# Four graph layers on one core: the small steps of the norms on GpSimd, a two-pass exponential unit, and new ranks

## The chip, the core and the metric

The kernel runs on one core of a Trainium2 chip. The core has a TensorE for matrix products (PE in the profile, with its weight loads shown apart as PEld), a VectorE (DVE), a ScalarE (ACT), a GpSimd (POOL) and a SyncE (SP). The engines run side by side; each works through its own queue of instructions in order, and they wait for each other by semaphores. The metric is the device time of one execution in microseconds (us), as the median of several runs. The profile is of one execution.

## The reference

The input is 16 graphs of 1024 nodes with 128 features each, and a 1024x1024 matrix of edges per graph. Four attention layers follow each other. After each one comes a residual sum and a layer norm:

```python
def _layernorm(x, axis=-1, eps=1e-5):
    m = jnp.mean(x, axis=axis, keepdims=True)
    v = jnp.var(x, axis=axis, keepdims=True)
    return (x - m) / jnp.sqrt(v + eps)
...
x = _layernorm(x + _L0_gnn_ref(x, adj, ...), axis=-1)
x = _layernorm(x + _L1_gnn_ref(x, adj, L1_gnn_W, L1_gnn_a), axis=-1)
x = _layernorm(x + _L2_gnn_ref(x, adj, ...), axis=-1)
x = _layernorm(x + _L3_gnn_ref(x, adj, L3_gnn_W, L3_gnn_a), axis=-1)
```

The third of them holds two attention steps, each behind a graph norm, and each ends in an exponential linear unit (elu); the first of the two has eight heads:

```python
def graph_norm(x, alpha, scale, shift, num_features):
    ...
    var = mean_x2 - mean * mean
    xn = (xr - alpha[None, :, None] * mean) / jnp.sqrt(var + EPS)
    xn = scale[None, :, None] * xn + shift[None, :, None]
...
h = graph_norm(x, gn1_alpha, gn1_scale, gn1_shift, nfeat)
h = gat_layer(h, adj, W1, a1, nheads, n_hidden1, concat=True)
h = graph_norm(h, gn2_alpha, gn2_scale, gn2_shift, nhid)
out = gat_layer(h, adj, W2, a2, 1, nhid, concat=False)
```

So each graph passes six norms: four layer norms and two graph norms. Each of them needs one over the root of a variance.

## The kernel before

A graph's 1024 nodes lie on 128 partitions in 8 groups, so that a tile of a whole graph is 128 x 1024 values. The sixteen graphs are sixteen passes through the function `graph(b)`, but nothing runs in the order in which it is written. A recorder (`Recorder`) takes down each operation with its engine, its operands and what it depends on. `Recorder.run` then works through a plan: every operation has a rank, every engine a time at which it is free, and at each step the operation that can start first is taken, with the lowest rank where two can. Operations of up to four graphs (`AHEAD = 3`) may be mixed. For operations made with `either`, such as copies from PSUM, the scaling by a row's factor (`scaled_rows`) or the affine pass of a norm (`affine`), the plan also chooses between ScalarE and VectorE. `Recorder.issue` then writes the instructions down in the planned order, so each engine's queue is fixed before the kernel starts. All these instructions carry line 430 in the profile; they are told apart by the names of their tiles.

The ranks are an operation's place in its graph, plus the graph's number times `STEP`, plus corrections from tables: `SHIFT` (by place in the graph), `OWN` (by graph and place), `ENDS` (by graph), `LATER` and `LAST` (a handicap on choosing one engine over the other). The plan uses an estimate of each operation's cost (`cost_of`); an arithmetic step on GpSimd of n elements per partition stands there with 200 + 2n ns in which the engine is held.

The places that the change touches:

- `rstd_of` computes one over a root for n variances per partition: ScalarE's Ln and Exp give a first value in `rs_r` (or in `last`, for the last norm of a graph), and three VectorE steps on `rs_q` refine it. It serves all six norms.
- `layernorm` (tiles `ln_m`, `ln_d`, `ln_v`, `shift`) stands behind the first and the third layer. From the statistics of each row in `mv`, which VectorE's bn_stats writes for the two halves of a row, it makes mean and variance in five VectorE steps, calls `rstd_of`, makes `shift` and hands over to eight affine passes.
- `layernorm_centred`, behind the second and the fourth layer, takes sums of squares `ss` from ScalarE, calls `rstd_of` and scales. In the last graph the fourth layer's is split into three pieces.
- The first graph norm (tiles `mvg`, `ga`, `gb`, 128x1) has four VectorE steps after `rstd_of`; the second (tiles `mom`, `var`, `ga8`, `gb8`, 128x8, which appear as `ga` and `gb` in the profile) has two ahead of it and four after it.
- The exponential unit of the eight heads works on `h2`, one 128 x 1024 tile per graph.

Between the norms lie the wide operations of VectorE, 128 x 1024 or 128 x 512 each: the products of weights and mask (`weights_of`: `row<-row,ratio,maskT`), the comparisons of the eight heads (`row<-row,ns`, which either engine can do), their masking (`row<-row,maskT`) and the sums over PSUM (`x<-bank`).

GpSimd has next to no arithmetic in this kernel. Its queue carries 36 DMA issues: eight that load the first two graphs' edges, and for each of the other fourteen graphs one that brings the edges over as bf16 (`adj<-in_adj_dram`) and one that loads the turned mask into its place (`maskT<-up`). The queue of SyncE carries the other transfers.

Of the kernel before, what the change touches and what calls it, by code (L numbers as in the profile page):

```python
# [21 lines left out]
P = 128  # L22
# [419 lines left out]
def gnn_stack_kernel(ctx: ExitStack, tc: tile.TileContext, w: dict, out: bass.AP):  # L442
# [11 lines left out]
    def fast_path(stack):  # L454
# [70 lines left out]
        for count in (1, D):  # L525
            eps[count] = const([P, 1], f"eps{count}")
            nc.vector.memset(eps[count], count * EPS)
# [81 lines left out]
        def rstd_of(var, n, r=None, count=1):  # L609

            if r is None:
                r = small("rs_r", P, n)
            q = small("rs_q", P, n)
            rc.scalar.activation(r, var, AF.Ln, bias=eps[count])
            rc.scalar.activation(r, r, AF.Exp, scale=-0.5)
            rc.vector.scalar_tensor_tensor(q, var, count * EPS, r, ALU.add, ALU.mult)
            rc.vector.scalar_tensor_tensor(q, q, -0.5 * count**0.5, r, ALU.mult, ALU.mult)
            rc.vector.scalar_tensor_tensor(r, q, 1.5 * count**0.5, r, ALU.add, ALU.mult)
            return r
# [4 lines left out]
        def layernorm(y, bs, r=None):  # L624
            twice, apart, var = (small(k, P, G) for k in ("ln_m", "ln_d", "ln_v"))
            rc.vector.tensor_tensor(twice, bs[:, :, 1], bs[:, :, 4], ALU.add)
            rc.vector.tensor_tensor(apart, bs[:, :, 1], bs[:, :, 4], ALU.subtract)
            rc.vector.scalar_tensor_tensor(apart, apart, D / 4.0, apart, ALU.mult, ALU.mult)
            rc.vector.tensor_tensor(var, bs[:, :, 2], bs[:, :, 5], ALU.add)
            rc.vector.tensor_tensor(var, var, apart, ALU.add)  # L630
            r = rstd_of(var, G, r, count=D)
            shift = small("shift", P, G)
            rc.vector.scalar_tensor_tensor(shift, twice, -0.5, r, ALU.mult, ALU.mult)
            for g in range(G):
                affine(y[:, g, 0:D], y[:, g, 0:D], r[:, g : g + 1], shift[:, g : g + 1])
# [206 lines left out]
        def graph(b):  # L842
# [147 lines left out]
            rc.vector.tensor_mul(ga, r, gn1[1])  # L990
            rc.vector.tensor_mul(gb, mv[:, 0:1], gn1[0])
            rc.vector.tensor_mul(gb, gb, ga)
            rc.vector.tensor_sub(gb, gn1[2], gb)
# [133 lines left out]
            rc.scalar.activation(e, h2, AF.Exp)  # L1127
            rc.vector.tensor_scalar(e, e, 1.0, -1.0, ALU.min, ALU.add)
            rc.vector.tensor_tensor(h2, h2, e, ALU.max)
# [12 lines left out]
            rc.vector.tensor_mul(var, mom[:, 0, :], mom[:, 0, :])  # L1142
            rc.vector.tensor_sub(var, mom[:, 1, :], var)
# [3 lines left out]
            rc.vector.tensor_mul(ga, r, gn2[:, 1, :])  # L1147
            rc.vector.tensor_mul(gb, mom[:, 0, :], gn2[:, 0, :])
            rc.vector.tensor_mul(gb, gb, ga)
            rc.vector.tensor_sub(gb, gn2[:, 2, :], gb)  # L1150
# [59 lines left out]
        for b in range(B):  # L1210
# [6 lines left out]
        LATER = {"vector": (122, -69, 156), "scalar": (66, -208, -6827)}  # L1217
        SHIFT = (
            3, 0, 12, -14, -124, -168, -37, -11, 130, -700, -702, -314, 104, 102, -282, -141, -150, -37, -23, -27,
            21, 27, 12, -23, 6, 47, 87, 193, 224, -183, -20, -6, 390, -479, -81, -387, 48, 56, 154, -4330,  # L1220
        )
        OWN = (
            (-1898, -1727, -871, -373, -2236, -1762, -2185, -2227, -1860, 872, -624, -909, 177, 153, -623, -117, 558, 649, -286, -733, -82, -35, 163, 158, 6, 62, -280, -413, -74, 85, -88, 244, -310, -830, -1150, -1555, -1749, -1397, -1363, -2273),
            (-740, -395, -86, 141, -113, -170, -67, -413, -471, -2323, -3056, -3903, -754, -1217, -892, -93, 644, 659, 392, 154, 484, -304, 291, 73, 14, -23, -183, -471, 139, 45, -54, -100, -299, -549, -786, -333, -137, -562, -375, 540),
            (-244, -188, -35, 102, -5, 18, -46, 79, 113, 337, -1213, -146, -286, 163, -81, 192, 583, 988, 78, -104, 5, 106, 140, 49, 23, 257, 76, 143, 1205, -237, 59, 45, 47, -186, -27, -215, -204, 136, 24, 664),
            (-1, 0, 16, 11, -24, -24, -28, -260, -232, -433, -306, -220, -204, -180, -167, -111, -193, -183, 37, 50, 2, 27, 26, 23, 13, 43, 45, 30, -25, 96, -7, -103, 608, 23, 263, 106, -52, 23, 61, 272),
            (8, 8, -6, -6, -13, 32, -7, 30, 30, -51, -38, -600, 5, 4, -23, -3, 15, 4, -15, 14, -5, -7, 12, 34, 131, 69, 68, 180, 31, 35, 101, 76, 9, -284, -291, -342, -367, -67, 11, -60),
            (21, 21, 23, 24, 23, 59, 63, 75, -39, -85, 89, -1235, -1221, -1138, 145, -90, -209, -109, 29, -250, -140, -115, 102, 306, 66, 20, -5, 1, -10, -175, 24, 17, -47, 29, 46, -1093, -356, -62, 11, 1),
            (-4, 5, 0, 0, 0, -97, 0, 68, 80, 30, 86, 56, 111, -25, 293, 134, 135, 49, 110, 128, -398, -290, 32, 33, 120, 13, -7, 18, 24, -21, -168, -163, -3, -87, -45, -77, -3, -9, -39, 16),
            (1, -3, -3, -13, -1, 24, -16, -17, -158, -54, -144, -22, 9, -1, -1, -8, -8, -1, 0, 18, -141, 14, 16, 53, 37, -57, -14, -26, -19, -23, -30, -38, -65, -369, -133, 0, -45, -30, -39, 854),  # L1230
            (0, 0, 0, 9, 1, -16, -53, -52, 298, -27, -45, -240, -93, -304, -296, -272, -246, -194, -192, -109, 9, -42, -47, -27, -29, -63, -11, 2, -1, -11, -58, -39, -20, -21, -223, -231, -324, -376, -417, -116),
            (1, -2, -970, 0, 0, -26, -44, -43, 25, -1104, -1179, -19, -451, -637, -839, -694, -19, 68, 30, 32, -8, -11, -55, 337, 351, -2, 17, 8, 4, -8, 38, 38, -2, -10, -95, -866, -839, -1062, -615, -790),
            (-6, -6, -29, -43, -47, -157, -1, -16, 91, 32, 20, -27, -17, -215, -35, -165, -226, -234, -232, -3, -3, -32, -54, 8, -38, -116, -46, 1, 6, 178, 198, 224, 153, 203, -15, -245, -146, -1139, -1245, -2114),
            (-43, -43, -51, -51, -33, -38, 28, 61, -49, -827, -930, -2108, 334, -4, 75, -41, -23, 21, -37, -63, 52, 49, 53, 9, 50, -80, 28, 41, -57, 66, 57, 20, -141, 112, 31, -668, -705, 338, 347, 421),
            (-20, 20, 6, 1, -12, -7, 78, 11, -39, -704, 10, 55, -41, -269, -66, -188, 41, 54, 19, 14, 67, 141, 47, 28, 12, 7, 11, 25, 35, 51, -7, -38, 7, -5, 256, -18, -189, -885, 89, -471),
            (-318, -303, -137, -102, -154, -319, -2367, -2650, -2247, -1733, -7880, -8504, -1388, -1036, 708, 568, -120, 613, 434, 1065, 5085, 2400, -4970, -3152, 885, 1161, 239, 406, 331, 1441, 4292, 3547, -1664, 709, 4888, 6934, 5929, 5348, 10822, 10232),
# [658 lines left out]
```

## Time and profile before

| what | value |
|---|---|
| median of 3 runs | 2430.28 us (2427.98 to 2431.34) |
| the profiled execution | 2428.53 us, of which the span of the trace is 2426.4 us |
| granted TensorE clock | 0.990 |
| VectorE, three-input products `row<-row,ratio,maskT` 128x1024 | 384 instructions, 469.0 us, 1274 ns each |
| VectorE, masking `row<-row,maskT` 128x2048 uint16 | 256 instructions, 309.1 us, 1213 ns each |
| VectorE, comparisons `row<-row,ns` 128x1024 | 308 instructions, 221.4 us, 741 ns each |
| ScalarE, the same comparisons `row<-row,bs2h` 128x1024 | 716 instructions, 767.5 us, 1142 ns each |
| VectorE, a step of `rstd_of` on 128x8 | 64 instructions, 10.1 us, 158 ns each |
| VectorE, `ln_d<-mv` 128x8 | 32 instructions, 5.3 us, 165 ns each |
| GpSimd, 128x1 copy | 2 instructions, 184 ns each |

A page of the profile gives for each engine its busy time, the share of the span and the number of instructions, then the span in 40 slices with the busy share in tenths. Three slices' lines of that page:

```profile
PE   8999999999999999999999999999999999999987
ACT  5597876949679596877859689596876959768864
POOL 1000000000000000000000000000000000000000
```

Every slice is about 61 us long. PE shows 9 nearly everywhere, that is 90% or more; ScalarE swings between 5 and 9; GpSimd is busy only in the first slice. A busy PE need not run at its peak, since the ends of matmuls are modelled.

### The profile page before, as it was taken

The numbers are of one execution on the slowest core, as the hardware profiler recorded it, in microseconds if no ns is written. First come the engines' busy times: TensorE is split into PE (matmuls) and PEld (weight loads), VectorE is DVE, ScalarE is ACT, GpSimd is POOL, SyncE is SP. The second block draws the span as 40 slices with busy tenths as digits, with TensorE's granted clock in tenths as the row PEclk, the third lists the DMA queues.
The fourth block names the chain that finished last, engine by engine and source line by source line (L and its number), as shares of the span: only waits on it lengthen the run. The fifth ranks groups of instructions, "written<-read, shape, count | busy, mean of one in ns | idle before, by whom it ended". The sixth has DMA issues, their size and how long they took to land.

```text
span 2426.4 us, 56241 instructions
## 1 busy us (share of the span) xinstructions
PE 2338.0 (96%) x23100; PEld 1995.4 (82%) x23100; DVE 2258.5 (93%) x4858; ACT 1832.5 (76%) x3451; POOL 28.7 (1%) x47
## 2 busy tenths in 40 slices
PE   8999999999999999999999999999999999999987
PEld 5786887969978797887879878798788978879887
DVE  5799998989999999999999999999999999999997
ACT  5597876949679596877859689596876959768864
POOL 1000000000000000000000000000000000000000
PEclk9999999999999999999999999999999999999999
DMA  9560235062072432607135080442605224020200
GB/s 202 115 171 10 80 90 147 10 148 80 19 191 46 120 100 72 165 19 176 50 81 149 29 207 20 111 108 67 170 19 142 77 80 108 17 79 2 71 2 28
DMA packets 215544, 217.20 MB, mean 90 GB/s; under 512 B 126264, under 2 KB 162288, under 8 KB 213488
## 3 DMA queue, kind: packets, MB, share of 16 engines
q1 hardware_dynamic: 197552, 165.30, 23.7%
q0 software_dynamic: 17728, 48.24, 10.5%
q8 instruction: 183, 3.00, 0.5%
q14 instruction: 81, 0.66, 0.1%
HBM read 193.94 MB, written 67.79 MB: 108 GB/s over the span
## 4 chain that ended last, share of the span: by engine, by line
PE 52%; DVE 40%; ACT 4%; issue 3%; DMA 1%; POOL 0%; ACTq 0%; DVEq 0%
PE bank L430 52%; DVE row L430 27%; DVE x L430 6%; ACT row L430 4%; DVE mv L430 1%; DVE m L430 1%; DVE mf L430 1%; DVE bank L430 1%; DMA row<-in_adj_dram 1%; DVE top_all L430 0%; DVE rdens L430 0%; DVE sums L430 0%; DVE rs_q L430 0%; DVE top L430 0%; DVE ln_v L430 0%
## 5 line engine op out<-in xcount | busy, mean ns | idle before, releaser
L430 PE MATMUL bank<-row,row 128*128 128x129 f32 (+1 forms) x9220 | 1421.4, 313 | 19.8 <-DVE row L430 14.0
L430 PEld LDWEIGHTS bank<-row,row 128*128 128x128 f32 x9220 | 1116.5, 192 | 210.2 <-issue 137.9
L430 ACT ACTIVATE row<-row,bs2h 128x1024 fp8e4<-128x1024 f32 x716 | 767.5, 1142 | 0.0
L430 DVE SCALAR_TENSOR_TENSOR row<-row,ratio,maskT 128x1024 f32<-128x1024 f32 x384 | 469.0, 1274 | 2.6 <-PE bank L430 2.4
L430 PEld LDWEIGHTS <-row 128*128 128x128 fp8e4 (+1 forms) x8320 | 413.2, 98 | 53.4 <-issue 24.2
L430 PE MATMUL bank<-m,row 128*128 128x102 bf16 x8192 | 427.6, 208 | 14.0 <-DVE row L430 12.6
L430 DVE TENSOR_TENSOR row<-row,maskT 128x2048 uint16<-128x2048 uint16 x256 | 309.1, 1213 | 1.7 <-ACT row L430 1.6
L430 ACT ACTIVATE row<-bank 128x512 f32<-128x512 f32 x256 | 150.8, 593 | 169.8 <-DVE bank L430 155.7
L430 DVE TENSOR_SCALAR row<-row,ns 128x1024 fp8e4<-128x1024 f32 x308 | 221.4, 741 | 0.0
L430 PE MATMUL bank<-m,maskT 128*128 128x136 bf16 x3072 | 209.5, 225 | 2.4 <-DVE m L430 2.3
L430 PEld LDWEIGHTS <-maskT 128*128 128x128 fp8e4 x3072 | 200.3, 97 | 4.6 <-issue 4.1
L430 DVE COPY_PREDICATED bank<-maskT,bank 128x512 f32<-128x512 uint8 x256 | 175.7, 689 | 29.5 <-PE bank L430 28.4
L430 DVE CUSTOM_DVE_ANT_0 row<-bank,row 128x512 f32<-128x512 f32 x256 | 173.6, 683 | 9.9 <-ACT row L430 8.6
L430 DVE TENSOR_REDUCE x<-bank 128x136 f32<-128x408 f32 x256 | 144.5, 571 | 12.3 <-PE bank L430 11.7
L430 ACT ACTIVATE row<-bank,rdens 128x128 f32<-128x128 f32 x206 | 60.5, 364 | 113.6 <-DVE rdens L430 113.1
L430 ACT ACTIVATE row<-row,top_all 128x1024 f32<-128x1024 f32 x128 | 139.4, 1144 | 4.7 <-DVE top_all L430 4.6
L430 ACT ACTIVATE half<-maskT,minus_half 128x2048 fp8e4<-128x2048 fp8e4 x64 | 127.5, 1996 | 0.2
L430 PE MATMUL bank<-ident,row 128*128 128x128 f32 x643 | 103.2, 285 | 20.6 <-ACT row L430 11.1
L430 PEld LDWEIGHTS bank<-ident,row 128*128 128x128 f32 x643 | 75.5, 143 | 52.3 <-ACT row L430 21.4
L430 ACT ACTIVATE sq<-row 128x128 f32<-128x128 f32 x256 | 76.4, 302 | 45.7 <-DVE row L430 43.2
L430 ACT COPY row<-bank 128x512 f32<-128x512 f32 x125 | 69.2, 580 | 21.4 <-PE bank L430 20.9
L430 DVE TENSOR_TENSOR row<-row,row 128x384 f32<-128x384 f32 (+3 forms) x120 | 69.8, 587 | 5.4 <-ACT row L430 4.6
(200 smaller groups left out, 2195.7 us busy)
## 6 DMA issues: line engine op xcount, KB each, us to landing
row<-s1d SPq DMA_DIRECT2D x128, 512.0 KB
adj<-in_adj_dram POOLq DMA_DIRECT2D x14, 2048.0 KB, 27.7
up<-half SPq DMA_DIRECT2D x112, 256.0 KB
row<-a_d SPq DMA_DIRECT2D x39, 512.0 KB
maskT<-up POOLq DMA_DIRECT2D x14, 1024.0 KB, 10.5
row<-in_x_dram SPq DMA_DIRECT2D x16, 512.0 KB
out_dram<-row SPq DMA_DIRECT2D x15, 512.0 KB
row<-in_adj_dram POOLq DMA_DIRECT2D x8, 512.0 KB, 16.1
```

What stands on the lines that cost most here:

```text
L430: done = getattr(getattr(self.nc, engine), name)(*[real(a) for a in args], **{k: real(a) for k, a in kw.items()})
```

## The change

It has three parts.

1. The small steps of the norms move from VectorE to GpSimd. VectorE's fused steps (`scalar_tensor_tensor`: a scalar operation and then one with a second tensor) become plain products and sums, so there are more of them: `rstd_of` has five in place of three, with a new tile `rs_v`; `layernorm` has seven ahead of `rstd_of` in place of five. For this the variance is now scaled so that `rstd_of` runs with `count=4` in place of `count=D`, with a constant of its own in `eps`. Ln and Exp stay on ScalarE.
2. The exponential unit of the eight heads was Exp on ScalarE and two passes on VectorE (a minimum and a sum, then a maximum). It becomes Relu of the negated value and Exp of the negated result on ScalarE, and one pass on VectorE.
3. All rank tables have new values, with the sizes as before.

```diff
-        for count in (1, D):
+        for count in (1, 4, D):
...
+            held = small("rs_v", P, n)
             q = small("rs_q", P, n)
+            rc.gpsimd.tensor_scalar(held, var, count * EPS, None, ALU.add)
             rc.scalar.activation(r, var, AF.Ln, bias=eps[count])
             rc.scalar.activation(r, r, AF.Exp, scale=-0.5)
-            rc.vector.scalar_tensor_tensor(q, var, count * EPS, r, ALU.add, ALU.mult)
-            rc.vector.scalar_tensor_tensor(q, q, -0.5 * count**0.5, r, ALU.mult, ALU.mult)
-            rc.vector.scalar_tensor_tensor(r, q, 1.5 * count**0.5, r, ALU.add, ALU.mult)
+            rc.gpsimd.tensor_tensor(q, held, r, ALU.mult)
+            rc.gpsimd.tensor_tensor(q, q, r, ALU.mult)
+            rc.gpsimd.tensor_scalar(q, q, -0.5 * count**0.5, 1.5 * count**0.5, ALU.mult, ALU.add)
+            rc.gpsimd.tensor_tensor(r, q, r, ALU.mult)
...
-            rc.vector.tensor_tensor(twice, bs[:, :, 1], bs[:, :, 4], ALU.add)
-            rc.vector.tensor_tensor(apart, bs[:, :, 1], bs[:, :, 4], ALU.subtract)
-            rc.vector.scalar_tensor_tensor(apart, apart, D / 4.0, apart, ALU.mult, ALU.mult)
-            rc.vector.tensor_tensor(var, bs[:, :, 2], bs[:, :, 5], ALU.add)
-            rc.vector.tensor_tensor(var, var, apart, ALU.add)
-            r = rstd_of(var, G, r, count=D)
+            rc.gpsimd.tensor_tensor(apart, bs[:, :, 1], bs[:, :, 4], ALU.subtract)
+            rc.gpsimd.tensor_tensor(var, bs[:, :, 2], bs[:, :, 5], ALU.add)
+            rc.gpsimd.tensor_tensor(apart, apart, apart, ALU.mult)
+            rc.gpsimd.tensor_scalar(var, var, 4.0 / D, None, ALU.mult)
+            rc.gpsimd.tensor_tensor(var, var, apart, ALU.add)
+            rc.gpsimd.tensor_tensor(twice, bs[:, :, 1], bs[:, :, 4], ALU.add)
+            rc.gpsimd.tensor_scalar(twice, twice, -0.5, None, ALU.mult)
+            r = rstd_of(var, G, r, count=4)
             shift = small("shift", P, G)
-            rc.vector.scalar_tensor_tensor(shift, twice, -0.5, r, ALU.mult, ALU.mult)
+            rc.gpsimd.tensor_tensor(shift, twice, r, ALU.mult)
...
-            rc.vector.tensor_mul(ga, r, gn1[1])
-            rc.vector.tensor_mul(gb, mv[:, 0:1], gn1[0])
-            rc.vector.tensor_mul(gb, gb, ga)
-            rc.vector.tensor_sub(gb, gn1[2], gb)
+            rc.gpsimd.tensor_mul(ga, r, gn1[1])
+            rc.gpsimd.tensor_mul(gb, mv[:, 0:1], gn1[0])
+            rc.gpsimd.tensor_mul(gb, gb, ga)
+            rc.gpsimd.tensor_sub(gb, gn1[2], gb)
...
-            rc.scalar.activation(e, h2, AF.Exp)
-            rc.vector.tensor_scalar(e, e, 1.0, -1.0, ALU.min, ALU.add)
-            rc.vector.tensor_tensor(h2, h2, e, ALU.max)
+            rc.scalar.activation(e, h2, AF.Relu, scale=-1.0)
+            rc.scalar.activation(e, e, AF.Exp, scale=-1.0)
+            rc.vector.scalar_tensor_tensor(h2, e, -1.0, h2, ALU.add, ALU.max)
...
-            rc.vector.tensor_mul(var, mom[:, 0, :], mom[:, 0, :])
-            rc.vector.tensor_sub(var, mom[:, 1, :], var)
+            rc.gpsimd.tensor_mul(var, mom[:, 0, :], mom[:, 0, :])
+            rc.gpsimd.tensor_sub(var, mom[:, 1, :], var)
...
-        LATER = {"vector": (122, -69, 156), "scalar": (66, -208, -6827)}
+        LATER = {"vector": (127, -141, 77), "scalar": (76, -220, -8863)}
         SHIFT = (
...
```

The four steps after `rstd_of` in the second graph norm (`ga8`, `gb8`) change in the same way as those of the first. `AHEAD` and `STEP` keep their values.

## The prediction

> **What bounds the kernel now.** I read the page's totals and slices first, then the middle of the span as one stretch, the chain of waits, the groups by shape, and last the timelines of VectorE and GpSimd at two norms and at GpSimd's DMA issues.
>
> ```profile
> PE 2338.0 (96%) x23100; PEld 1995.4 (82%) x23100; DVE 2258.5 (93%) x4858; ACT 1832.5 (76%) x3451; POOL 28.7 (1%) x47
> PE 52%; DVE 40%; ACT 4%; issue 3%; DMA 1%; POOL 0%; ACTq 0%; DVEq 0%
> 180.00:2160.00 1980.00, 1933.22 (x19093) 1640.81 (x19090) 1884.79 (x4031) 1514.81 (x2860) 18.97 (x23) 1.00 0.35 92
> ```
>
> The third line is a stretch's length, then busy PE, PEld, DVE, ACT and POOL. Between 180 and 2160 us PE idles 1980 - 1933 = 47 us and DVE 95 us: two full engines, with ACT a quarter free and POOL empty. The chain that ended last alternates: 52% on PE, 40% on DVE. So DVE time is worth something, but only where DVE heads the chain; I price it at 0.40 and keep 1.0 as the upper end. PE's idle 47 us is about what a better order alone could win there.
>
> **1. What leaves VectorE.** The instruction lists of the two built programs give the counts: DVE 5848 to 5210, POOL 80 to 985, ACT 3536 to 3503, PE and SP unchanged. Removed from DVE are 40 small steps per graph: 9 in each of two layernorms, 3 in each of four further rstd, 4 and 6 in the two graph norms. 16 x 40, and 6 for the last graph's two extra pieces, make 646. Their price is not the mean of some 157 ns:
>
> ```profile
> 1487.29 0.16 DVE L430 TENSOR_TENSOR ln_m<-mv 128x8 f32<-128x8 f32 x1
> 1487.37 0.17 DVE L430 TENSOR_TENSOR ln_d<-mv 128x8 f32<-128x8 f32 x1
> 1487.45 0.25 DVE L430 TENSOR_TENSOR ln_v<-mv 128x8 f32<-128x8 f32 x2
> 1487.62 0.16 DVE L430 SCALAR_TENSOR_TENSOR ln_d<-ln_d 128x8 f32<-128x8 f32 x1
> ```
>
> Columns are start, duration, engine and operation. Starts are 0.08 us apart: each instruction overlaps the next by 0.08. So 646 x 0.08 = 52 us leave DVE, not 101. The exponential unit drops one 128x1024 TENSOR_SCALAR per graph (689 ns by its row, 0.61 net of overlap): 16 x 0.61 = 10 us. Where two engines can do a step, the new ranks choose anew: DVE takes 22 more 128x1024 comparisons (0.66 net each, 15 us), 21 more 128x384 products (0.47, 10 us) and 10 more 128x512 biases (6 us), and gives up 17 casts (11 us) and some copies; together about +19. DVE ends 52 + 10 - 19 = 43 us lighter; on the path 0.40 x 43 = **-17 us** (ends: 0 and -43).
>
> **2. What ScalarE gets.** One more 128x1024 pass per graph (Relu, 1055 ns by the row of the same shape, 16 us in all); against it 22 comparisons and 65 products leave, and casts come: about zero in sum on an engine with a quarter free. As a dependence, Relu and Exp and one DVE pass replace Exp and two DVE passes: 1.06 - 0.69 = +0.37 us per graph, 6 us in all, 0.40 of it **+2 us**.
>
> **3. What GpSimd gets.** The count per graph is 13 steps in each of two layernorms, 5 in each of four rstd, 4 and 6: 56, and 10 for the last graph, so 906 in all. No such step is in this trace. The nearest rows are a 128x1 COPY on POOL, 184 ns, and the same step on DVE, 157 ns; in the empty tail three dependent DVE steps start 0.19 and 0.20 us apart. Alone, a step on POOL should take 0.2 to 0.25 us, and a layernorm that waited 5 us behind wide DVE work (1486.8 to 1491.9) would be done in 3 to 4: POOL's queue is otherwise empty. That is the case for the change. Against it stand these rows:
>
> ```profile
> 1427.68 0.54 POOL L430 DMA_DIRECT2D maskT<-up  x1 [127.89 <-DVE x L430]
> 1428.21 1.27 POOL L430 DMA_DIRECT2D adj<-in_adj_dram  x1
> ...
> 1428.31 0.72 DVE L430 CAST m<-x 128x1088 bf16<-128x1088 f32 x1
> ...
> 1297.87 1.04 POOL L430 DMA_DIRECT2D maskT<-up  x1 [162.09 <-ACT row L430]
> ...
> 1297.38 1.40 DVE L430 TENSOR_SCALAR row<-row,ns 128x1024 fp8e4<-128x1024 f32 x2
> ...
> 1719.90 1.47 POOL L430 DMA_DIRECT2D adj<-in_adj_dram  x1 [0.62 <-issue]
> ...
> 1720.23 1.04 DVE L430 CAST m<-x 128x1088 bf16<-128x1088 f32 x1
> ```
>
> GpSimd's issue of maskT takes 0.54 us where nothing is in the way and that of adj 0.89. The long ones lie on a DVE CAST or TENSOR_SCALAR, and end 0.1 to 0.5 us after it; in the last pair the CAST too is long, 1.04 against a usual 0.72. So the two engines already hold each other up, in both directions.
>
> How often would it strike? CAST and TENSOR_SCALAR of this kind are busy 246 us, 10% of the span. DVE operations that read two SBUF tiles (469.0, 309.1, 41.1, 41.0, 39.9, 39.0 and 35.2 us in their groups) are 974 us, 40%. Whether these collide with a POOL step no row shows, since a DMA issue is not an arithmetic step that reads tiles. I count them in, as the nearer case for a reading step: 50%.
>
> (a) Hold of DVE: half of the steps meet such an operation, and I let each hold the next one for half a COPY: 906 x 0.5 x 0.092 = 42 us, on the path 0.40 x 42 = **+17 us**. Ends: nothing, and every step a whole COPY, 906 x 0.184 = 167 us, at 0.40 67 us.
>
> (b) Lateness of POOL: the 1220 us in question are some 1200 instructions, 1.0 us each; a step that meets one waits half of it: 906 x 0.5 x 0.5 = 227 us, 2.4 us for each of 96 norms. Behind a late norm ACT's Ln and its scaling passes wait at the head of their queue, DVE's scaling passes too, and then PE's transposes. How much reaches the end? ACT idles 594 us in this trace, nearly all of it in waits, and PE 47 us in the middle: 8%. So 0.08 x 227 = **+18 us** (ends: nothing, and 0.40 x 227 = 91 us).
>
> The Trainium skill's page "SBUF — State Buffer", section "Who interferes with whom", speaks against this change: a VectorE instruction that reads two SBUF tensors contends with a GpSimd instruction that reads SBUF, and one in a two-port mode always does; whichever comes second waits for the whole of the other. The rows above bear out the two-port half alone. By those rows alone, with 10% in place of 50%, (a) and (b) shrink to about 6 us and the sum would be near 2423; by the page's whole-instruction lock, with a full COPY of hold, (a) doubles and the sum is near 2469.
>
> **4. Queues and ends.** POOL's queue carries 36 DMA issues, which now stand between norms. A maskT issue waits for its landing and a free place, so the next graph's norm stands behind it, and the issue stands behind a norm. The first matters little where both come in the planned order (issue 0.54 and 0.89 us, 28 of them, 20 us of POOL in all); the second is covered: maskT issued at 1297.9 is first read by a copy-predicated at 1387. SP's queue keeps its 567 instructions. In the last graph nothing covers a norm; six of them with one or two more steps of 0.2 us make **+2 us**. The new ranks reorder every engine; nothing here prices that, so 0, between -47 (PE's idle in the middle gone) and +47.
>
> **Sum:** -17 + 2 + 17 + 18 + 2 = +22 us on the profiled execution, 2428.5 us (span 2426.4 and 2.1 around it): 2450.5. The median of the runs is 1.8 us above that execution: **2452 us**.
>
> **The rivals.**
>
> - *No contention (faster).* POOL steps run free, as nothing in the trace shows an arithmetic step held. Then (a) and (b) go: -17 + 2 + 2 = -13, or -43 if DVE is worth its full time and norms come sooner: 2387 to 2420, about 2410. For it: DVE's 95 us idle in the middle against PE's 47, and 5-us norms in DVE's queue. Against it: the stretched issues. It decides as soon as (a) and (b) cost less than 13 us together.
> - *Locked out (much slower).* POOL doesn't get between back-to-back DVE instructions and waits for the end of a run, such as eight 128x1024 products in 9.65 us at 1462.49. Two half runs per norm, 96 x 9.6 = 926 us, at 0.2 of it on the path: +185, about 2610. For it: the issue at 1297.87 lasts beyond the second of two TENSOR_SCALARs. Against it: one row is no proof, and its last writes may have come late.
> - *Nothing to tell.* Relief and holds cancel: 2430. The runs before spread by 0.14%, so 0.2%, or 5 us, is about what a measurement tells from no change.
> - That the change does not do what it says is excluded: the lists show 646 steps gone from DVE and 906 on POOL.
>
> **How the numbers follow.** Contention as summed 0.47, locked out 0.09, no contention 0.35, nothing 0.09. The time is that of the first. Its own range is 2436 (holds and lateness at half) to 2530 (either near its upper end). The range over the cases, 2398 to 2525, leaves out most of the locked-out case and the far ends of two others. Slower 0.47 + 0.09 = 0.56, same 0.09, faster 0.35.
>
> **What would show it.** In the changed profile: DVE's busy time near 2258 - 43 + 42, that is not falling by 43; the 128x1024 two-tile products longer than 1274 ns, and comparisons longer than 741; POOL steps with durations of 0.3 to 1.2 us instead of 0.2; ACT and DVE waits that end on POOL tiles (shift, rs_r, ga, gb, last). I am wrong if POOL steps stay near 0.2 us with DVE's rows unchanged: then the time should be near 2410.

## The result and the profile after

The changed kernel takes **2483.86 us** (median of 4 runs, 2482.12 to 2485.12) against 2430.18 for the kernel before, timed beside it: 1.0221 times as long [1.0204, 1.0239]. It was forecast at 2452. The sign came out, and the time lies in the range, but the loss is 54 us where 22 were summed. The profiled execution took 2483.71 us, of which the span is 2481.8. (One execution of the kernel E1 below ran at a granted clock of 0.749 and took 2976.66 us; its median leaves that one out.)

These are the page's totals, the chain that ended last, and the stretch from 180 to 2160 us, in the columns of the prediction's first fence:

```profile
PE 2357.8 (95%) x23100; PEld 2007.5 (81%) x23100; DVE 2217.2 (89%) x4220; ACT 1830.3 (74%) x3418; POOL 316.5 (13%) x953
PE 53%; DVE 31%; ACT 5%; POOL 5%; issue 3%; DMA 2%; POOLq 0%; ACTq 0%; DVEq 0%
180.00:2160.00 1980.00, 1902.78 (x18779) 1618.96 (x18776) 1815.88 (x3441) 1487.27 (x2764) 254.81 (x774) 0.99 0.37 90
```

VectorE did become lighter, 2258.5 to 2217.2 us, that is by 41 us where 43 were worked out. Yet in the middle stretch its idle time grew from 95 to 164 us and PE's from 47 to 77. VectorE's share of the chain fell from 40% to 31%, and GpSimd, which had none, now holds 5%. The freed time became waiting.

Not all of the longer span is waiting, though. PE's busy time grew by 19.8 us, to 2357.8, for the same 23100 matmuls, and its idle time by 35.6. The granted clock of the TensorE fell from 0.990 to 0.983. If PE's work went in proportion to that clock, the difference would be worth some 17 us (an estimate from these two figures and the span). The kernels below show the like: 0.983 to 0.986 in all that lose 34 us and more in a kept order, 0.988 to 0.991 in the others. No run holds the clock fixed, so its part of the loss is not known; the prediction had no term for it.

The groups that GpSimd was feared to slow (count, busy time, mean ns of one, idle time ahead):

```profile
L430 DVE SCALAR_TENSOR_TENSOR row<-row,ratio,maskT 128x1024 f32<-128x1024 f32 x384 | 468.3, 1270 | 0.1
...
L430 DVE TENSOR_TENSOR row<-row,maskT 128x2048 uint16<-128x2048 uint16 x256 | 308.5, 1211 | 14.6 <-ACT row L430 14.1
L430 DVE TENSOR_SCALAR row<-row,ns 128x1024 fp8e4<-128x1024 f32 x330 | 235.1, 739 | 2.2 <-DMA out_dram<-row 1.9
```

1270, 1211 and 739 ns stand against 1274, 1213 and 741 before, and back-to-back products start 1.196 us apart with a GpSimd step beside them or without: VectorE's wide operations are not held up. The new waits are those of ScalarE and VectorE for GpSimd (us in total, times, longest); the last line is one of before:

```profile
ACT rs_r L430 <- POOL ln_v L430: 44.0, 19, 5.7
...
ACT row L430 <- POOL shift L430: 15.9, 17, 2.6
ACT row L430 <- POOL last L430: 14.5, 10, 4.2
...
DVE row L430 <- POOL shift L430: 19.0, 19, 3.6
...
ACT rs_r L430 <- DVE ln_v L430: 1.7, 4, 0.6
```

Before, ScalarE's Ln (`rs_r`) waited 1.7 us in all for VectorE's `ln_v`, and its scaling passes 3.3 us for `shift` and 18.2 for `last`. One such wait in the timeline (start, duration, operation, in brackets the idle time ahead and what ended it):

```profile
352.62 3.48 DVE L430 TENSOR_TENSOR row<-row,maskT 128x2048 uint16<-128x2048 uint16 x3
352.66 3.53 POOL L430 TENSOR_SCALAR rs_v<-ss 128x8 f32<-128x8 f32 x1 [36.68 <-ACT sq L430]
...
356.27 0.20 POOL L430 TENSOR_TENSOR rs_q<-rs_v,last 128x8 f32<-128x8 f32 x1
...
357.36 1.28 ACT L430 ACTIVATE row<-row,last 128x128 f32<-128x128 f32 x4 [4.21 <-POOL last L430]
```

A step of 0.20 us takes 3.53, as long as the three maskings that VectorE runs meanwhile, and ScalarE stands still for 4.21 us behind it. I counted the 906 steps in the trace: the median is 0.20 us, 141 of them (16%) last over 0.3 us, the longest 5.71, and what they last beyond 0.21 us adds up to 116 us. In some 95 of the 141 one VectorE operation ends within the step, in some 46 two to five do (a few change sides with how an operation is counted that ends just as the step begins).

These steps now lie on the path. In the chain that ended last the small steps of the norms add up to 24 us before, all on VectorE, and to 116 us after, all on GpSimd (added up over the pieces of the chain, tile by tile).

### The profile page after: what moved, and what is told of

It is laid out like the page before. It is cut to its first block, busy times and chain, and to the rows that moved or that the text cites. A ratio compares the mean times of both kernels' runs of the same rounds, so it can differ in the third digit from the quotient of the medians.

```text
span 2481.8 us, 56606 instructions
## 1 busy us (share of the span) xinstructions
PE 2357.8 (95%) x23100; PEld 2007.5 (81%) x23100; DVE 2217.2 (89%) x4220; ACT 1830.3 (74%) x3418; POOL 316.5 (13%) x953
## 4 chain that ended last, share of the span: by engine, by line
PE 53%; DVE 31%; ACT 5%; POOL 5%; issue 3%; DMA 2%; POOLq 0%; ACTq 0%; DVEq 0%
PE bank L430 53%; DVE row L430 21%; ACT row L430 4%; DVE x L430 4%; DVE bank L430 1%; POOL ln_d L430 1%; DVE m L430 1%; DVE mv L430 1%; POOL rs_q L430 1%; POOL ln_v L430 1%; DVE mf L430 1%; DMA out_dram<-row 1%; DMA row<-in_adj_dram 1%; DMA s1d<-s1t 1%; POOL ln_m L430 0%
## 5 line engine op out<-in xcount | busy, mean ns | idle before, releaser
L430 PE MATMUL bank<-row,row 128*128 128x129 f32 (+2 forms) x9220 | 1433.8, 313 | 18.8 <-DVE row L430 9.7
L430 PEld LDWEIGHTS bank<-row,row 128*128 128x128 f32 x9220 | 1125.6, 192 | 219.6 <-issue 151.1
L430 ACT ACTIVATE row<-row,bs2h 128x1024 fp8e4<-128x1024 f32 x694 | 742.9, 1142 | 7.0 <-DVE x L430 5.0
L430 DVE SCALAR_TENSOR_TENSOR row<-row,ratio,maskT 128x1024 f32<-128x1024 f32 x384 | 468.3, 1270 | 0.1
L430 PEld LDWEIGHTS <-row 128*128 128x128 fp8e4 (+1 forms) x8320 | 421.7, 99 | 53.8 <-issue 29.5
L430 PE MATMUL bank<-m,row 128*128 128x102 bf16 x8192 | 443.0, 209 | 14.4 <-DVE row L430 10.2
L430 DVE TENSOR_TENSOR row<-row,maskT 128x2048 uint16<-128x2048 uint16 x256 | 308.5, 1211 | 14.6 <-ACT row L430 14.1
L430 DVE TENSOR_SCALAR row<-row,ns 128x1024 fp8e4<-128x1024 f32 x330 | 235.1, 739 | 2.2 <-DMA out_dram<-row 1.9
L430 ACT ACTIVATE row<-bank 128x512 f32<-128x512 f32 x256 | 148.1, 592 | 112.2 <-DVE bank L430 103.3
L430 PE MATMUL bank<-m,maskT 128*128 128x136 bf16 x3072 | 210.0, 225 | 4.0 <-DVE m L430 3.5
L430 DVE COPY_PREDICATED bank<-maskT,bank 128x512 f32<-128x512 uint8 x256 | 174.3, 687 | 42.8 <-PE bank L430 41.7
L430 PEld LDWEIGHTS <-maskT 128*128 128x128 fp8e4 x3072 | 199.4, 97 | 9.0 <-issue 8.5
L430 DVE CUSTOM_DVE_ANT_0 row<-bank,row 128x512 f32<-128x512 f32 x256 | 171.1, 680 | 15.3 <-ACT row L430 14.0
L430 PE MATMUL bank<-ident,row 128*128 128x128 f32 x643 | 113.2, 291 | 42.9 <-ACT row L430 25.4
L430 DVE TENSOR_REDUCE x<-bank 128x136 f32<-128x408 f32 x256 | 143.2, 569 | 11.6 <-PE bank L430 11.4
L430 ACT ACTIVATE row<-row,top_all 128x1024 f32<-128x1024 f32 x128 | 138.3, 1138 | 6.4 <-DVE top_all L430 6.2
L430 PEld LDWEIGHTS bank<-ident,row 128*128 128x128 f32 x643 | 77.4, 146 | 70.5 <-ACT row L430 34.5
L430 ACT ACTIVATE half<-maskT,minus_half 128x2048 fp8e4<-128x2048 fp8e4 x64 | 127.7, 1999 | 0.1
L430 POOL TENSOR_TENSOR ln_d<-mv 128x8 f32<-128x8 f32 x32 | 25.6, 800 | 775.7 <-DVE mv L430 604.3
L430 ACT ACTIVATE sq<-row 128x128 f32<-128x128 f32 x256 | 76.5, 301 | 56.0 <-DVE row L430 52.6
L430 ACT ACTIVATE row<-bank,rdens 128x128 f32<-128x128 f32 x141 | 42.0, 365 | 92.2 <-DVE rdens L430 92.2
L430 ACT ACTIVATE row<-row 128x1024 f32<-128x1024 f32 x48 | 50.7, 1055 | 63.8 <-DVE row L430 47.9
```

The lines of the kernel that those rows point to most:

```text
L430: done = getattr(getattr(self.nc, engine), name)(*[real(a) for a in args], **{k: real(a) for k, a in kw.items()})
```

## The experiments

Two theories: the steps on GpSimd are late because VectorE's wide operations hold them; or the loss lies elsewhere, in the longer chains of plain steps or in the new order. The tables of ranks make this hard to part, since they fix the order of everything.

### Parts of the change, with the order planned anew or kept

E1 keeps the changed kernel's order, decided with the steps on GpSimd, and sends the 906 steps to VectorE at the moment of issue. E2 is the kernel before with the new exponential unit alone, E3 the change with the old tables, E4 the kernel before with the new tables; these three plan their order anew.

```diff
# E1, in Recorder.issue of the changed kernel
-                todo += [(way[0], *call) for call in way[2]]
+                move = way[0] == "gpsimd" and way[1] not in ("dma_start", "tensor_copy")
+                todo += [("vector" if move else way[0], *call) for call in way[2]]
...
# E2, in the kernel before
-            rc.scalar.activation(e, h2, AF.Exp)
+            rc.scalar.activation(e, h2, AF.Relu, scale=-1.0)
+            rc.scalar.activation(e, e, AF.Exp, scale=-1.0)
...
# E4, in the kernel before (E3 the other way round, in the changed kernel), and the other tables likewise
-        LATER = {"vector": (122, -69, 156), "scalar": (66, -208, -6827)}
+        LATER = {"vector": (127, -141, 77), "scalar": (76, -220, -8863)}
```

> The changed kernel's planned order, kept exactly, but the 906 arithmetic steps are issued on VectorE at the places where the plan has them. Lateness theory (POOL steps held behind runs of wide VectorE operations make the norms late): the held time of the steps goes, and 906 x 0.08 = 72 us of VectorE work comes back, about 0.4 of it on the path; between 2435 and 2460 us. Order theory (the new ranks are a worse order on the chip, wherever the steps run): 2484 and more, up to 2510, since VectorE only gets more to do.

> The kernel before with the new exponential unit alone, old ranks. Lateness theory: no part in the loss, 2420 to 2440. If the extra ScalarE pass is what costs: 2450 or more.

> The change with the rank tables of before. Lateness theory: still slow, 2470 to 2520, since the steps on POOL are held as before. Order theory: back near 2430.

> The kernel before with the rank tables of the change. Lateness theory: 2420 to 2450. Order theory: 2470 or more.

E1: 2487.04 us, 1.0236 [1.0216, 1.0257] times the kernel before, as the order theory had it. With the same plain steps in the same order VectorE does as badly as GpSimd, 3.2 us apart, although it is busy 2300.2 us then, 83 more than in the changed kernel. E2: 2724.2, E3: 3111.13, E4: 2999.89. These three are misses: a table of ranks fits one exact set of operations, and with any other the plan it gives is 12 to 28% worse (1.1204 [1.1185, 1.1222] for the mildest). They say nothing of what the parts cost. So every later run keeps an order whole and changes only what is issued at an operation's place.

### The old order kept

E5 moves the norms' steps to GpSimd in the old order, each of the 358 fused steps as two plain ones, 1004 in all by the trace (the expectations say 992). E6 puts in the new exponential unit alone, E7 both. E12, a later one, issues the same 1004 plain steps on VectorE. With E5 and the changed kernel and E1 this makes two pairs that differ in the engine alone.

```diff
# E5 (E12: "vector" in place of "gpsimd"), in the kernel before; Recorder.issue and `instead` alike in E5 to E12
-                todo += [(way[0], *call) for call in way[2]]
+                swap = self.ops[i].swap
+                todo += swap if swap is not None else [(way[0], *call) for call in way[2]]
...
+        def instead(op, *calls):
+            op.swap = [(engine, name, args, kw) for engine, name, args, kw in calls]
...
+        def on_pool(op):
+            _, (call,) = op.ways[0][0], op.ways[0][2]
+            name, args, kw = call
+            if name != "scalar_tensor_tensor":
+                return instead(op, ("gpsimd", name, args, kw))
+            o, a, c, b, op0, op1 = args
...
+            return instead(
+                op, ("gpsimd", "tensor_scalar", (t, a, c, None, op0), {}),
+                ("gpsimd", "tensor_tensor", (o, t, t if a is b else b, op1), {}),
+            )
...
# E6
-            rc.scalar.activation(e, h2, AF.Exp)
+            instead(rc.scalar.activation(e, h2, AF.Exp), ("scalar", "activation", (e, h2, AF.Relu), dict(scale=-1.0)))
...
```

> The planned order of the kernel before, kept exactly on every engine, but all 646 small norm steps are issued on GpSimd in plain products and sums (992 steps, since each fused one becomes two), at the places where the plan has them. If the move to GpSimd is what costs (steps held behind wide VectorE runs, late norms): 2460 to 2510. If the move is harmless or good and the new planned order costs: 2405 to 2440.

> The planned order of before, kept, with the new exponential unit at the old one's places (the second operation goes to ScalarE in place of VectorE). Harmless by both theories: 2422 to 2440. If the added ScalarE pass delays the norm behind it: 2440 to 2450.

> Both parts of the change in the old planned order. If costs add up: the sum of the two differences above. If the move is what costs: 2460 to 2515; if the new order is: 2405 to 2445.

> The planned order of before, kept, with the same 992 plain products and sums as e5, but on VectorE: 346 steps more there than before, 346 x 0.08 = 28 us. Against e5 only the engine differs. If it is the longer chains of plain steps that make the norms late: 2465 or more. If it is GpSimd (held steps, hand-over): 2435 to 2455.

| kernel | steps of the norms | median us | ratio [95%] | VectorE busy us | PE waits for `row` tiles, us |
|---|---|---|---|---|---|
| before | 646 fused on VectorE | 2430.2 | 1 | 2258.5 | 56.7 |
| E6 | the same, new exponential unit | 2431.85 | 1.0009 [0.9999, 1.0018] | 2249.4 | |
| E5 | 1004 plain on GpSimd | 2491.81 | 1.0253 [1.0236, 1.027] | 2214.4 | 103.0 |
| E12 | 1004 plain on VectorE | 2486.97 | 1.0241 [1.0223, 1.0259] | 2313.2 | 89.1 |
| E7 | E5 and E6 | 2488.78 | 1.0235 [1.0216, 1.0254] | 2204.9 | |
| after | 906 plain on GpSimd, new order | 2483.86 | 1.0221 [1.0204, 1.0239] | 2217.2 | 66.7 |
| E1 | 906 plain on VectorE, new order | 2487.04 | 1.0236 [1.0216, 1.0257] | 2300.2 | 68.1 |

The norms are the whole loss: +62 us, while the new exponential unit changes nothing that can be told. That speaks against the order theory. The changed kernel is 5 us below E7, with 98 steps fewer and with overlapping intervals, so the new ranks win little or nothing. And E12 loses 57 us with no step on GpSimd: splitting the steps is enough to lose as much. VectorE can be 99 us lighter (E12 to E5) and the time is not better for it. Why E12 loses is open in one point: its 358 additional steps make the norms' chains longer, and they also make VectorE 55 us busier. Its share of the chain that ended last rises from 40% to 52%:

```profile
DVE 52%; PE 38%; ACT 6%; issue 3%; DMA 1%; DVEq 0%; POOL 0%; ACTq 0%
```

No run parts the two on VectorE. In E5 VectorE is lighter and the chains are as long, but there the holds come in.

In the old order most of the lost time shows in PE's waits. First E5, then E12 (their lines are numbered one higher, L431 for L430), then before:

```profile
PE bank L431 <- ACT row L431: 51.9, 33, 4.2
PE bank L431 <- DVE row L431: 51.1, 52, 8.5
```

```profile
PE bank L431 <- DVE row L431: 44.9, 68, 3.0
PE bank L431 <- ACT row L431: 44.2, 37, 4.6
```

```profile
PE bank L430 <- DVE row L430: 30.6, 49, 2.6
PE bank L430 <- ACT row L430: 26.1, 24, 4.1
```

In the changed kernel these two grow by only 10 us in sum, so there this reading covers a small part. E5's part is not all of the norms either: VectorE's products wait 18.0 us in two places for the transfer that fills `row` from `a_d`, which they don't do before or in E12. The `row` tiles are what a norm's scaling passes write and PE transposes next; the group of these transposes (`bank<-ident,row`, 643 of them) idles 20.6 us before, 49.5 in E5, 45.9 in E12, 42.9 in the changed kernel.

As E5 and E12 have the old order, each norm can be laid against the same norm of the kernel before, in the two parts that can be matched: from a layernorm's first step to its Ln (32 of them), and from Exp to the refined root (98). In E12 nearly all are later, 76 us in sum; none is earlier to speak of. In E5 73 parts are later, by 65 us in sum, and 57 are earlier, by 54 us in sum; the sum of both is 11 us, and the end comes some 60 us later. (E5's sums move by up to some 10 us with where a part is taken to begin and end.) That would fit if what is late passes on and what is early is used by nobody, but it is argued and not shown. The chain that ended last says it more directly: the norms' small steps on it are 24 us before, 23 in E6, 99 in E12 and 135 in E5, so 74 and 111 us more in the two that end 57 and 62 us later.

### Fewer steps

The split lengthens the chain of dependent steps in each norm. Here it is shortened instead: the refining steps of `rstd_of` are left out, with the factor in Ln's scale. That leaves out a part of the computation, the refinement of the first value of one over the root. E8 and E11 use the old order (the remaining steps fused on VectorE, or 416 plain ones on GpSimd); E9 and E10 use the changed kernel's order (fused on VectorE, or the 416 on GpSimd).

```diff
# E8
-            rc.scalar.activation(r, var, AF.Ln, bias=eps[count])
+            rc.scalar.activation(r, var, AF.Ln, bias=eps[1], scale=1.0 / count)
...
-            rc.vector.scalar_tensor_tensor(q, var, count * EPS, r, ALU.add, ALU.mult)
+            instead(rc.vector.scalar_tensor_tensor(q, var, count * EPS, r, ALU.add, ALU.mult))
...
# E9, in the changed kernel
-            rc.gpsimd.tensor_tensor(shift, twice, r, ALU.mult)
+            instead(rc.gpsimd.tensor_tensor(shift, twice, r, ALU.mult), ("vector", "scalar_tensor_tensor", (shift, twice, -0.5, r, ALU.mult, ALU.mult), {}))
```

An `instead` with nothing behind the operation issues nothing at that place. E11 sends what E8 leaves through `on_pool`; E10 leaves out the five steps of `rstd_of` in the changed kernel.

> The planned order of before, with the three refining steps of each root left out (Ln with a scale of 1/count gives the root directly): 294 small VectorE steps less and nothing put in their place, so this is the relief of VectorE and of the norms' chains alone. 294 x 0.08 = 24 us of VectorE; at 0.4 of it on the path 2420, at all of it 2406; a chain shorter by three steps for 98 norms can add up to 10 us. If relief of VectorE is worth nothing in this order: 2430.

> The changed kernel's planned order, kept, with no arithmetic on GpSimd: the refinement of the roots is left out (Ln with a scale gives the root), and the other small steps are issued on VectorE in their old, fused forms. VectorE then carries about the 2236 us of e8, whose operations are the same but for the exponential unit, so the two differ in the planned order alone. If the new order is as good as the old one once the steps are on VectorE: 2410 to 2430. If the new order, made for steps on GpSimd, is a worse one by itself: 2450 to 2475.

> The change, its planned order kept, with the refinement left out: 416 of 906 GpSimd steps stay and nothing goes to VectorE. If the loss is lateness from GpSimd steps, it shrinks with their number: 2440 to 2465. If the order alone costs: 2475 to 2484. Against e9 it prices the 416 remaining steps on GpSimd.

> The planned order of before, refinement left out as in e8, the remaining small steps on GpSimd (some 416, fused ones as two). Against e8 (2420) it prices these steps alone. If the cost goes by the number of steps (62 us for 992): 2445 to 2450. If it is the wait of the norms however few the steps: 2460 or more. If GpSimd is harmless: 2415 to 2425.

| order | few steps, fused, on VectorE | 416 plain steps on GpSimd | all steps, plain, on GpSimd | all steps, plain, on VectorE |
|---|---|---|---|---|
| old | E8: 2420.11, 0.9953 [0.9936, 0.9971] | E11: 2430.59, 1.0006 [0.9996, 1.0016] | E5: 2491.81 | E12: 2486.97 |
| new | E9: 2446.05, 1.0067 [1.005, 1.0083] | E10: 2463.87, 1.0137 [1.0121, 1.0154] | after: 2483.86 | E1: 2487.04 |

In each row the time grows with the number of steps. (E11 came out below the 2445 to 2450 of a fixed price per step, and E9 lies between its two ranges.) Where the steps are few, GpSimd is the worse place: 10.5 us (E11 against E8) and 17.8 us (E10 against E9), with 23 and 27 us less on VectorE. That includes the split of the few fused steps which remain. In the new order E9 is 26 us slower than E8 although VectorE's busy time is within 7 us (2242.8 and 2235.6): the new order, taken by itself, is a worse one for short norms. And in the old order the 294 refining steps are worth 10 us (before to E8), 0.03 us each, while the 358 steps that the split adds (before to E12) cost 57, 0.16 each. It is as if the old order had room for the norms as long as they were, and little for longer ones. The norms' small steps on the chain that ended last go the same way: 12 us in E8, 35 in E11, 78 in E10. E8 is faster than both kernels, than the one before by 10 us, under half a percent.

### A step beside a run, by itself

After these runs I read the long steps in the trace as a rule: a GpSimd step is held until a whole run of wide VectorE operations is over. Only single places said so. E13 and E14 put a stretch ahead of the kernel before, in which a chain of 13 dependent 128x8 products on GpSimd runs beside one kind of VectorE operation. In E13 all operations of a run write one tile; in E14 each has its own. Their total times, 2501.9 and 2539.44 us in one run each, say nothing.

```diff
# E14, ahead of the kernel before (E13: the same `call` at each k, so one tile)
+        for _, count, call in kinds:
+            step("vector", "tensor_tensor", thin[0], thin[1], thin[2], ALU.mult)
+            step("gpsimd", "tensor_tensor", thin[3], thin[0], thin[0], ALU.mult)
+            for k in range(count):
+                c = call(k)
+                step("vector", *c[0:-1], **c[-1])
+            for _ in range(12):
+                step("gpsimd", "tensor_tensor", thin[3], thin[3], thin[3], ALU.mult)
+            step("vector", "tensor_tensor", thin[1], thin[3], thin[3], ALU.mult)
```

> The kernel before, with a stretch put ahead of it in which chains of dependent 128x8 products run on GpSimd (12 each, started together with VectorE) beside runs of one kind of VectorE operation: nothing; 8 of the three-input 128x1024 products; 8 comparisons 128x1024 from one tile to fp8; 8 maskings 128x2048 uint16; 8 one-tile 128x1024 f32 passes; 12 with one operand in PSUM; 40 short two-tile ones of 128x128. After that, small steps on VectorE alone: 12 dependent products, 12 dependent fused steps, 12 that don't depend on each other. The total time is some tens of us above 2430 and says nothing. Theory (a GpSimd step that meets an operation with two SBUF tiles or in a two-port mode is held until the whole run of them ends): beside products, maskings and the short two-tile run one GpSimd step lasts nearly the whole run (8 x 1.2 to 1.3 = 9 to 10 us) and the rest come after it at 0.28 us each; beside one-tile fp8 comparisons as well, if their mode is a two-port one; beside PSUM operands 0.2 us throughout. Rival (a step waits for the one operation that it meets, as the prediction had it): each of the 12 steps lasts 0.6 to 1.3 us beside products, none longer. Rival (no hold; the long steps are late dependences): all steps 0.2 us in every stretch. On VectorE: dependent small steps start 0.19 us apart, fused ones alike, independent ones 0.08 us apart.

> As the last run, but each VectorE operation of a run writes a tile of its own, as in the kernel, so that the next one starts 0.08 us before it ends; there all wrote one tile, each started 0.04 us after the one before had ended, and one GpSimd step came between every two (each 1.24 us beside products), while the products stood 1.32 us apart. Stretches: 8 products; 8 comparisons; 8 maskings; 8 one-tile passes; 8 with an operand in PSUM; 40 short two-tile ones; 8 products that write one tile, as before; 8 products in four pairs, each pair on one tile. Then 8 products twice with own tiles and 8 on one tile, with no GpSimd step. Theory (a GpSimd step gets in only where two operations of VectorE do not overlap): beside 8 products with own tiles the chain's second or third step lasts the whole rest of the run, some 9 to 10 us, and VectorE's run keeps its length without GpSimd, 9.65 us; maskings and one-tile passes alike, 9 and 5 us; in the pairs one step per pair, about 2.5 us each. Rival (a step waits for one operation only, and the long steps in the kernel's trace are late dependences): 1.1 to 1.3 us a step with own tiles too, and VectorE's products 1.3 us apart. The third stretch without GpSimd says what the step between two products costs VectorE: 1.32 less their distance there.

E13, beside the products, then beside operations with one operand in PSUM, then small steps on VectorE alone (dependent products, dependent fused steps, independent products):

```profile
11.56 1.28 DVE L532 SCALAR_TENSOR_TENSOR row<-row,mt,row 128x1024 f32<-128x1024 f32 x1
11.66 1.24 POOL L532 TENSOR_TENSOR mt<-mt 128x8 f32<-128x8 f32 x1
12.89 1.28 DVE L532 SCALAR_TENSOR_TENSOR row<-row,mt,row 128x1024 f32<-128x1024 f32 x1
12.99 1.24 POOL L532 TENSOR_TENSOR mt<-mt 128x8 f32<-128x8 f32 x1
...
50.39 0.20 POOL L532 TENSOR_TENSOR mt<-mt 128x8 f32<-128x8 f32 x1
...
71.62 2.44 DVE L532 TENSOR_TENSOR mt<-mt 128x8 f32<-128x8 f32 x13
73.98 2.36 DVE L532 SCALAR_TENSOR_TENSOR mt<-mt 128x8 f32<-128x8 f32 x12
76.26 1.00 DVE L532 TENSOR_TENSOR mt<-mt,mt 128x8 f32<-128x8 f32 x12
```

One step per product, held until that product is over: the rival of my theory, and what the prediction had assumed. But the products stood 1.32 us apart there and not 1.20, which left open whether a step gets through only at such a gap. E14 answers that. First the chain beside products with own tiles and beside maskings, then three runs of eight products on VectorE: on one tile beside GpSimd, with own tiles without it, on one tile without it:

```profile
8.87 1.09 POOL L533 TENSOR_TENSOR mt<-mt 128x8 f32<-128x8 f32 x1
10.03 1.12 POOL L533 TENSOR_TENSOR mt<-mt 128x8 f32<-128x8 f32 x1
11.23 1.12 POOL L533 TENSOR_TENSOR mt<-mt 128x8 f32<-128x8 f32 x1
...
26.14 1.06 POOL L533 TENSOR_TENSOR mt<-mt 128x8 f32<-128x8 f32 x1
27.28 1.06 POOL L533 TENSOR_TENSOR mt<-mt 128x8 f32<-128x8 f32 x1
...
55.84 10.53 DVE L533 SCALAR_TENSOR_TENSOR row<-row,mt,row 128x1024 f32<-128x1024 f32 x8
...
79.84 9.65 DVE L533 SCALAR_TENSOR_TENSOR row<-row,mt,row 128x1024 f32<-128x1024 f32 x8
...
99.50 10.52 DVE L533 SCALAR_TENSOR_TENSOR row<-row,mt,row 128x1024 f32<-128x1024 f32 x8
```

Here the products overlap as in the kernel, and still each step waits for one operation only. My theory of whole runs falls as a rule. The gap of 0.12 us belongs to VectorE writing one tile again (10.52 us without GpSimd, 10.53 with it): the steps cost VectorE nothing. But each step of the chain is held anew. Alone the steps start 0.28 us apart; the 13 took 3.5 us beside PSUM operands, 5.2 beside short two-tile operations of 128x128, 6.1 beside one-tile passes, 6.6 beside comparisons, 10.4 beside maskings. On VectorE dependent steps start 0.20 us apart, plain ones ((2.44 - 0.17 - 0.08) / 11, as the first of that line's 13 does not belong to the chain) and fused ones ((2.36 - 0.17) / 11), and independent ones 0.08.

The Trainium skill's page "SBUF — State Buffer", section "Who interferes with whom", says that the later of the two waits for the whole of the other's instruction, that a VectorE instruction with one SBUF input outside a two-port mode does not contend, and that one-tile `tensor_scalar` may run in such a mode. GpSimd's side of this agrees: 1.12 us beside products, 0.53 beside one-tile passes, 0.20 beside PSUM operands. That VectorE would wait in its turn these runs don't bear out: with small steps beside it its products start 1.20 us apart as without, and the measurement decides here.

## Why the prediction was right in sign and wrong in size

**What leaves VectorE (step 1).** 43 us forecast, 41 measured. Its worth, priced at 0.40 on the path, -17 us, is not borne out. With the same steps in the same order, 83 and 99 us of VectorE's time (after and E1, E5 and E12) were worth 3.2 and -4.8 us, net of what the steps suffer on GpSimd. E8 gained 10 us with 23 us less on VectorE, about the assumed 0.40, but its norms are shorter too, so the relief by itself was never measured.

**The exponential unit (step 2).** Forecast +2 on the path and -4 in the relief; measured +1.7, which can't be told from nothing.

**Hold of VectorE (step 3a).** Forecast +17, measured none, in the kernel's rows (1270 ns for 1274, starts 1.196 us apart) and in E14. The assumption that each engine holds the other is wrong for this pairing. The stretched CAST that the prediction read as a sign of it was beside a DMA issue, not an arithmetic step.

**Lateness of GpSimd (step 3b): here the step failed.** It has two factors. The waits were forecast at 227 us and were 116, so this factor was too large. The second, "ACT idles 594 us ... and PE 47 us in the middle: 8%", was far too small. On the chain that ended last the norms' small steps grew by 92 us, from 24 to 116, and the time by 54; in E5 it was 111 and 62, in E12 74 and 57, in E10 53 and 34. More than half reached the end there, not a twelfth; in E11, with the shortest chains on GpSimd, it was 11 and nothing. Leaving out 588 of E5's GpSimd steps (E11) took back 61 us. The matched parts give 60 of 65 in E5 and 57 of 76 in E12, an upper reading, since the early parts are not counted and not every part was matched. The share of idle time is an average over the whole span, but a late norm does not fall on average work: the scaling passes wait at the head of ScalarE's and VectorE's queues, nothing behind them may pass, and PE's transposes are next. The division of these us between holds and longer chains stays open.

**The longer chain was not a term at all.** The prediction counted that `rstd_of` has five steps for three and a layernorm thirteen for nine, but priced the extra ones only as load on an idle engine, and as +2 in the last graph. E12 prices the split alone: +57 us with every step on VectorE, its load there included. It splits more than the change does: behind Exp a root has three dependent steps before, six in E5 and E12, and four in the changed kernel, where the fifth step does not wait for Exp. The price of 0.08 us for a small step holds for independent ones; a chain pays 0.20 on VectorE and 0.28 on GpSimd.

**Ranks (step 4).** Forecast 0, between -47 and +47. E7 to after is -5 (with 98 steps fewer, hardly to be told from nothing), E8 to E9 +26: not one number, but dependent on how long the norms are.

**The rivals.** "No contention" had its own test, steps near 0.2 us and VectorE's rows unchanged. Both hold for most steps (84% under 0.3 us), yet the time is not near 2410: the test looked at the typical step, and missed the 16% that are held and the length of the chain. "Locked out" had a mechanism that occurs, some 46 steps that last over two to five operations, but is not the rule and costs far less than its 185 us.

**What stays open.** Whether a chain of plain steps on GpSimd without holds would win was not tried, since the holds can't be taken away while VectorE does its work. The 54 us can't be divided into holds, longer chains and order by adding: E12 loses by splitting alone as much as E5 does by splitting and holds beside a lighter VectorE. Nearest to a division come the steps within the changed kernel's own order: 20 us for the 490 refining steps (after to E10), 18 for having the other 416 on GpSimd and plain (E10 to E9), and 16 by which E9 still exceeds the kernel before. What the lower clock adds to the waits was not tried. Why a step in the kernel sometimes misses several gaps (about half of the 116 us) and never does in E14 was not found.

## What to carry to other kernels

Moving small steps off a full engine was paid for here in the time of their chain: the load fell as forecast and nothing was gained. So count the dependent steps, multiply by the start-to-start time of dependent steps on the new engine, add a hold for each step that meets a wide VectorE operation with its operands in SBUF (0.53 to 1.12 us in E14), and compare it with what the order has room for. In this fixed order more than half of what the norms' steps added to the chain that ended last came out in the time, where an average idle share had said 8%; that share was no measure of cover. Leaving dependent steps out gained where moving them lost: 10 us by E8 without a new order.

## What the hardware showed that was not expected

The contention was one-sided: 128x8 steps on GpSimd lasted 1.06 to 1.24 us beside 128x1024 products and maskings, while VectorE's run of eight products on one tile took 10.53 us with them and 10.52 without. Successive VectorE operations that write one tile start 1.32 us apart against 1.20 with tiles of their own, so a tile written again costs 0.12 us per 128x1024 product. And one-tile comparisons and passes hold GpSimd too (0.58 and 0.53 us a step), but operations with an operand in PSUM do not (0.20).
